# Pairing edge blocks on VectorE in a sparse graph-attention kernel

## The chip, the cores and the metric

The kernel runs on one core of a Trainium2 chip. A core has five engines that run their own queues in order: TensorE (PE in the profile, with its weight loads as PEld), VectorE (DVE), ScalarE (ACT), GpSimd (POOL) and SyncE (SP, which here only issues DMAs). The metric is the device time of one execution in microseconds, as the median over several runs; lower is better.

## The reference, cut to what matters

One layer of graph attention over 16 batches of 1024 nodes with 512 features and 8 heads of 64, followed by the residual and a layer norm. `adj` is the same for all batches, holds zeros and ones, and is sparse: few keys for most queries, many for some.

```python
q = (x @ Wq + bq).reshape(b, n, H, HD)
k = (x @ Wk + bk).reshape(b, n, H, HD)
v = (x @ Wv + bv).reshape(b, n, H, HD)
scores = jnp.einsum('bqhd,bkhd->bhqk', q, k) / jnp.sqrt(jnp.float32(HD))
scores = scores + (1.0 - adj)[None, None, :, :] * -1000000000.0
attn = jax.nn.softmax(scores, axis=-1)
out = jnp.einsum('bhqk,bkhd->bqhd', attn, v).reshape(b, n, d)
...
x = _layernorm(x + out @ Wo + bo)
```

All is float32.

## The kernel before, in words

**The sparse attention.** Instead of scores for all 1024 x 1024 pairs the kernel works on the edges alone. Queries are ranked by their number of keys and laid in 8 tiles of 128. A *block* is 128 edges: on each of the 128 partitions one query and one of its keys. `OWN = (2, 1, 2, 3, 4, 5, 5, 7)` gives the own blocks of each tile, where block i holds the i-th key of the tile's own 128 queries; `BLOCKS` adds one further block for tile 6 and five for tile 7, whose edges belong to arbitrary queries of the tile and are summed back by a matmul with a 0/1 matrix (`sums`). Some tiles with few keys are merged over two batches. In all there are 530 blocks, in the order of the list `blocks`; the blocks of neighbouring places mostly belong to one tile, with the further blocks spread in between.

**A block's life**, each step a function:
- `gather(n)` issues an indirect DMA on POOL that brings the 128 rows `kvg` (512 key and 512 value features, 4 KB a partition) from a table in DRAM; queries come as `qt`, once a tile through SP, or as `qg` for a further block, once a block through POOL.
- `products(n)` (L1313) multiplies queries and keys on VectorE into a tile `qk`.
- `scores(n)` (L1317) sums the product over each head's 64 features on VectorE, 8 values a partition.
- `exponentials(n)` (L1328) takes their exponential on ACT, into the last 8 columns of `pv`.
- `weigh(n)` multiplies the values by it: on ACT in eight pieces (L1341) or on VectorE at once (L1345). `by_act` chooses; 450 blocks go to ACT, 80 to VectorE.
- `add_own(n)` (L1357, VectorE) adds an own block to its tile's sum, or `add_up(n)` (L1366, L1367, PE) does it for a further block.
- `normalise` (L1387, VectorE) divides after a tile's last block, and the result goes through transposes (L1401) to the product with Wo (`po`, L799).

**The dense part.** For the batches to come, PE transposes x (`pxT`, L757) and makes q (`pq`, L799) and, for two tiles of x at a time, k and v by a Strassen-like scheme (L956) with banks `x`, `z` and `pp`; VectorE evacuates and combines (L783 to L786, L972, L975, L979, L984, L988), and ACT evacuates others (L761, L835, L969). The banks `x` and `z` have one buffer each, so the second use of `z` follows the evacuation at L984.

**The order** is written out by hand in one loop over steps n (L1538 to L1623), one block a step, with every engine's instructions issued in this order. In step n stand, one after the other: the exponential of block n + 3, the product of n + 4, the gathers up to n + 8 (11 near the end), VectorE's weighing of n + 1, the addition of n, the sum by heads of n + 4, the normalising of a tile that closed, what was put off to this step (`plan`: evacuations and parts of the layer norm), ACT's weighing of n + 2, more put-off work (`rest`), and then as many units of dense PE work as a running credit allows. Buffers are handed out in rotation by tag: tag "kvg" has 8 buffers of 4 KB a partition, which first hold the 8 tiles of `adj` while the edges are found; tag "kv" has 5, which serve the dense part, and edge blocks too near the end; "qk" has 2 of 2 KB.

A gather into a buffer waits for the weighing that read it last. POOL works in order, so what stands behind a waiting gather waits too.

Of the kernel before, what the change touches and what calls it, by code (L numbers as in the profile page):

```python
# [10 lines left out]
F32 = mybir.dt.float32  # L11
# [3 lines left out]
OP = mybir.AluOpType  # L15
AX = mybir.AxisListType

HEADS = 8
# [8 lines left out]
OWN = (2, 1, 2, 3, 4, 5, 5, 7)  # L27
# [11 lines left out]
PAIRED_FROM, SPARED = 2, 56  # L39
# [35 lines left out]
P = 128  # L75
# [103 lines left out]
def kernel(  # L179
# [36 lines left out]
    nc = tc.nc  # L216
    B, N, D = x.shape
    HD = D // HEADS
    NPAIR = D // P
# [35 lines left out]
    with ExitStack() as main:  # L255
# [380 lines left out]

        def edges(t):
            nb, J, K = BLOCKS[t], DEGREE[t], OWN[t]
            tag, bufs = ("kvg", KG_BUFS) if J > 16 else ("kv", 5)
            v = work.tile([P, N], F32, tag=tag, name=f"codes_{t}", bufs=bufs)  # L640
# [60 lines left out]
            for i0 in range(0, nb, step):  # L701
                n = min(step, nb - i0)
                g0 = first[t] + i0
                pg = fill_psum(f"pe_{t}_{i0}")
                g = pg[:, 0:n * (J + 3)].rearrange("p (n j) -> p n j", n=n)
                for i in range(n):
                    nc.tensor.matmul(g[:, i, :], of[:, ts(i0 + i, P)], kl, start=True, stop=True)
                yield
                e = small.tile([P, 2, n], F32, tag=f"ee{n}", name=f"ee_{t}_{i0}", bufs=1)
                m = work.tile([P, D], F32, tag="qk", name=f"em_{t}_{i0}", bufs=2)[:, 0:n * J].rearrange("p (n j) -> p n j", n=n)  # L710
                nc.vector.tensor_tensor(e[:, 0, :], placed[:, i0:i0 + n], g[:, :, J], op=OP.subtract)
                nc.vector.tensor_tensor(
                    m, place[:, None, 0:J].to_broadcast([P, n, J]), e[:, 0, :, None].to_broadcast([P, n, J]),
                    op=OP.is_equal,
                )
# [485 lines left out]

        KG, QG, PV, PSUM, QT, RDEN, V1 = {}, {}, {}, {}, {}, {}, {}

        def blocks_of(b, t):

# [42 lines left out]
        def gather(n):  # L1250
# [33 lines left out]
            else:  # L1284
# [7 lines left out]
            nc.gpsimd.indirect_dma_start(  # L1292
                out=KG[n], out_offset=None, in_=rows,
# [3 lines left out]

        S = {}

        QK = {}  # L1300

        def products(n):
            b, t, i = blocks[n]
            if t == 0 and i == 0 and b < PAIRED_FROM:
                norms = small.tile([P, NPAIR], F32, tag="lone", name=f"lone_{b}", bufs=1)
                later_last(0, lambda q=QT[b, t]: squares(f"q_{b}", q, norms, lone))
                later(2, lambda: nc.vector.tensor_reduce(lone_norm[:, b:b + 1], norms, axis=AX.X, op=OP.max))
            if i < OWN[t]:
                q = QT[b, t] if i < OWN[t] - 1 else QT.pop((b, t))
            else:  # L1310
                q = QG.pop(n)
            QK[n] = work.tile([P, D], F32, tag="qk", name=f"qk_{n}", bufs=2)
            nc.vector.tensor_tensor(QK[n], q, KG[n][:, 0:D], op=OP.mult)  # L1313

        def scores(n):
            S[n] = small.tile([P, HEADS], F32, tag="s", name=f"s_{n}", bufs=4)
            nc.vector.tensor_reduce(S[n], QK.pop(n).rearrange("p (h d) -> p h d", d=HD), axis=AX.X, op=OP.add)  # L1317

        def exponentials(n):

            b, t, i = blocks[n]
            if i == 0:
                PV[n] = work.tile([P, D + HEADS], F32, tag="pv0", name=f"pv_{n}", bufs=3)
            else:
                PV[n] = work.tile([P, D + HEADS], F32, tag="pv", name=f"pv_{n}", bufs=PV_BUFS)
            at = NK + i if t == 0 and merged(b) else own[t] + i
            bias = absent[:, at:at + 1] if i < OWN[t] else 0.0
            nc.scalar.activation(PV[n][:, D:], S.pop(n), AF.Exp, bias=bias)  # L1328
# [187 lines left out]
        with tc.manual_schedule():  # L1516
# [21 lines left out]
            while n < total or plan or rest or urgent or done or finishing or spilled or lone_tiles or not guarded:  # L1538
# [6 lines left out]
                elif n in start:  # L1545
# [112 lines left out]
```

## Time and profile before

| | us |
|---|---|
| median of 3 runs | 1860.07 |
| lowest and highest run | 1853.99, 1872.71 |
| span of the profiled execution, first to last instruction | 1840.4 |
| the profiled execution's own time | not shown; the runs lie 13.6 to 32.3 above the span |
| VectorE: products, L1313, both forms (x530) | 363.0 |
| VectorE: sums by heads, L1317 (x530) | 360.7 |
| VectorE: additions, L1357 (x329) | 228.3 |
| ACT: weighing, L1341 (x3600) | 907.5 |

The profile's line of a group reads: line, engine, operation, output and inputs by the program's tile names, shapes as partitions x elements, count, then busy time in all, mean of one in ns, and the engine's idle time just before such instructions with what ended it. Busy time of a group is what it adds to the time in which the engine has an instruction running, so where one instruction starts before the last has ended, count times mean is more than busy. The granted clock is the share of full clock that TensorE was given; its mean is 0.996.

### The profile page before, as it was taken

How to read it: one execution, taken by the hardware profiler on the slowest of the kernel's cores; microseconds unless marked ns; L12 is line 12 of the kernel's file. 1: busy time of each engine (PE TensorE's matmuls, PEld its weight loads, DVE VectorE, ACT ScalarE, POOL GpSimd, SP SyncE). 2: the span in 40 equal slices, each digit the busy share in tenths (PEclk: the TensorE clock that was granted, in tenths of full speed). 3: DMA queues.
4: the chain of work that ended last, by engine and by line, in shares of the span. 5: the costliest groups of instructions: out<-in, count | busy, mean ns of one | idle time of the engine just before them, and what ended most of it. 6: DMA issues, size and time to landing. Idle time of an engine off the chain costs nothing.

```text
span 1840.4 us, 25352 instructions
## 1 busy us (share of the span) xinstructions
PE 1798.2 (98%) x5140; PEld 876.2 (48%) x5140; DVE 1693.7 (92%) x3473; ACT 1563.2 (85%) x6183; POOL 1215.3 (66%) x1142
## 2 busy tenths in 40 slices
PE   7999999999999999999999999999999999999997
PEld 3444454554444454444444445444544444444443
DVE  6889889999989999999999999999999999997986
ACT  3637869989889898999889988989799999987886
POOL 1367766766565776767757666677666767665786
PEclk9999999999999999999999999999999999999998
DMA  7358787989889899999988998999989999889995
GB/s 287 106 190 253 256 325 237 346 301 327 308 280 314 295 336 319 344 316 308 347 316 310 346 335 276 343 321 322 339 315 325 314 355 326 306 324 325 338 319 191
DMA packets 198791, 558.54 MB, mean 303 GB/s; under 512 B 33450, under 2 KB 33470, under 8 KB 198626
## 3 DMA queue, kind: packets, MB, share of 16 engines
q0 software_dynamic: 112640, 370.50, 59.3%
q1 hardware_dynamic: 82910, 180.52, 26.2%
q10 hardware_dynamic: 3076, 5.82, 0.9%
q14 instruction: 122, 1.00, 0.2%
q8 instruction: 43, 0.70, 0.2%
HBM read 420.30 MB, written 157.45 MB: 314 GB/s over the span
## 4 chain that ended last, share of the span: by engine, by line
PE 69%; DVE 10%; ACT 9%; DMA 4%; issue 3%; POOL 1%; SPq 0%; POOLq 0%; DVEq 0%; ACTq 0%
PE po L799 17%; PE pq L799 15%; PE pp L956 12%; PE z L956 9%; PE x L956 9%; ACT pv L1341 5%; DVE qk L1313 2%; PE poT L1401 2%; PE pxT L757 2%; PE sum L1367 2%; DVE s L1317 2%; PE sum L1366 2%; DVE pv L1357 1%; ACT sq_k L809 1%; DMA kvg<-kv_pair,place_row 1%
## 5 line engine op out<-in xcount | busy, mean ns | idle before, releaser
L1341 ACT ACTIVATE pv<-kvg,pv 128x64 f32<-128x64 f32 x3600 | 907.5, 341 | 0.0
L1292 POOL DMA_INDIRECT kvg<-kv_pair,place_row x462 | 526.7, 1140 | 307.4 <-ACT pv L1341 99.6
L799 PE MATMUL pq<-wq,xT 128*128 128x512 f32 x792 | 367.8, 596 | 0.0
L1317 DVE TENSOR_REDUCE s<-qk 128x8 f32<-128x512 f32 x530 | 360.7, 681 | 6.8
L799 PE MATMUL po<-wo,oT 128*128 128x512 f32 x792 | 359.3, 594 | 0.7 <-ACT oT L1405 0.7
L1313 DVE TENSOR_TENSOR qk<-qt,kvg 128x512 f32<-128x512 f32 x434 | 297.2, 685 | 1.1 <-DMA kvg<-kv_rows,key_row 0.6
L956 PE MATMUL x<-b,xT 128*128 128x512 f32 x504 | 237.3, 593 | 0.5 <-ACT e L969 0.4
L956 PE MATMUL pp<-t,s 128*128 128x512 f32 x504 | 237.0, 593 | 0.0
L1357 DVE TENSOR_TENSOR pv<-pv,pv 128x520 f32<-128x520 f32 x329 | 228.3, 694 | 4.3 <-ACT pv L1341 4.2
L799 PEld LDWEIGHTS po<-wo,oT 128*128 128x128 f32 x792 | 149.1, 191 | 170.0 <-issue 160.2
L799 PEld LDWEIGHTS pq<-wq,xT 128*128 128x128 f32 x792 | 148.4, 192 | 161.9 <-issue 149.9
L1010 POOL DMA_INDIRECT x<-in_x_dram,asked_row x120 | 133.0, 1108 | 77.8 <-issue 21.3
L1148 POOL DMA_INDIRECT out_dram<-y,asked_row x129 | 146.9, 1139 | 39.1 <-issue 21.2
L1328 ACT ACTIVATE pv<-s,absent 128x8 f32<-128x8 f32 x434 | 127.0, 294 | 44.0 <-DVE s L1317 40.8
L809 ACT ACTIVATE sq_k<-kv 128x128 bf16<-128x128 f32 x512 | 150.8, 301 | 6.4 <-DVE kv L979 3.4
L956 PEld LDWEIGHTS pp<-t,s 128*128 128x128 f32 x504 | 94.7, 191 | 108.1 <-issue 99.4
L956 PEld LDWEIGHTS x<-b,xT 128*128 128x128 f32 x504 | 94.2, 191 | 107.4 <-issue 99.0
L956 PE MATMUL z<-b,s 128*128 128x512 f32 x252 | 119.2, 596 | 7.0 <-DVE kv L984 7.0
L1246 POOL DMA_INDIRECT qg<-q_rows,query_row x96 | 104.4, 1088 | 28.4 <-issue 26.9
L956 PE MATMUL z<-t,s 128*128 128x512 f32 x252 | 118.6, 593 | 0.0
L956 PE MATMUL pp<-t,xT 128*128 128x512 f32 x252 | 118.5, 593 | 0.0
L1134 ACT ACTIVATE y<-y,stats 128x512 f32<-128x512 f32 (+1 forms) x128 | 102.7, 806 | 17.0 <-DVE stats L1129 17.0
(279 smaller groups left out, 2713.0 us busy)
## 6 DMA issues: line engine op xcount, KB each, us to landing
kv_pair<-kv SPq DMA_DIRECT2D x98, 512.0 KB
q_rows<-q SPq DMA_DIRECT2D x106, 256.0 KB
qt<-q_rows SPq DMA_DIRECT2D x98, 256.0 KB
residual<-x SPq DMA_DIRECT2D x83, 256.0 KB
y<-residual SPq DMA_DIRECT2D x83, 256.0 KB
kv_rows<-kv SPq DMA_DIRECT2D x15, 512.0 KB
kvg<-kv_pair,place_row POOLq DMA_INDIRECT x462, 6.9
kv_pair<-kv SPq DMA_DIRECT2D x28, 256.0 KB
```

The costliest lines, as they stand in the source:

```text
L799: nc.tensor.matmul(p, lhs(c), w[:, c, :], start=(c == 0), stop=(c == NPAIR - 1))
L809: nc.scalar.activation(sq, s[:, ts(h, P)], AF.Square, scale=scale, accum_out=sums[:, h:h + 1])
L956: nc.tensor.matmul(R[bank], l[:, ts(c, P)], right[:, c, :], start=(first and c == 0), stop=(c == 1), skip_group_check=True,)
L1010: nc.gpsimd.indirect_dma_start(out=y, out_offset=None, in_=x_rows, in_offset=bass.IndirectOffsetOnAxis(ap=asked_row[:, t:t + 1], axis=0), ...
L1148: nc.gpsimd.indirect_dma_start(out=out_rows[b, t], out_offset=bass.IndirectOffsetOnAxis(ap=rows, axis=0), in_=y, in_offset=None, element_o ...
L1246: nc.gpsimd.indirect_dma_start(out=q, out_offset=None, in_=q_rows[b % ROWS], in_offset=bass.IndirectOffsetOnAxis(ap=rows, axis=0))
L1292: nc.gpsimd.indirect_dma_start(out=KG[n], out_offset=None, in_=rows, in_offset=bass.IndirectOffsetOnAxis(ap=(place_row if b else key_row)[ ...
L1313: nc.vector.tensor_tensor(QK[n], q, KG[n][:, 0:D], op=OP.mult)
L1317: nc.vector.tensor_reduce(S[n], QK.pop(n).rearrange("p (h d) -> p h d", d=HD), axis=AX.X, op=OP.add)
L1328: nc.scalar.activation(PV[n][:, D:], S.pop(n), AF.Exp, bias=bias)
L1341: nc.scalar.activation(pv[:, ts(h, HD)], v[:, ds(D + h * HD, HD)], AF.Copy, scale=pv[:, D + h:D + h + 1])
L1357: nc.vector.tensor_tensor(PV[b, t], PV[b, t], pv, op=OP.add)
```

## The change: blocks two at a time

Blocks 2m and 2m + 1 become a pair.

- Tag "kvg" now has 4 buffers for two blocks each (`PAIR`) in place of 8 single ones: the same memory. While dense work is left every pair lies in one such buffer; near the end two of three pairs do, and the others use two single "kv" buffers.
- `products` handles a pair: one multiplication of 128x1024 where both blocks use the same queries (broadcast over the two), else two of 128x512. The product is written over the keys in the gathered tile; the tiles `qk` are gone.
- `scores` handles a pair: one sum by heads over 128x1024 where the pair lies in one buffer.
- In the loop products and sums come in odd steps only, for blocks n + 3 and n + 4. So an even block's product comes one step later than before and an odd block's in the same step as before. Exponentials come one step later (n + 2), and VectorE's weighing stands before the gathers.
- The `adj` tiles, and the edge codes of the tile with most keys, use the paired buffers; a scratch tile of `edges` moves from tag "qk" to tag "ysq".

```diff
-KG_BUFS, Q_BUFS, QT_BUFS, PV_BUFS, Y_BUFS = 8, 5, 3, 5, 6
+KG_PAIRS, Q_BUFS, QT_BUFS, PV_BUFS, Y_BUFS = 4, 5, 3, 5, 6
...
-                ADJ.append(work.tile([P, N], F32, tag="kvg", name=f"adj_{t}", bufs=KG_BUFS))
+                if t % 2 == 0:
+                    two = work.tile([P, 2, N], F32, tag="kvg", name=f"adj_{t}", bufs=KG_PAIRS)
+                ADJ.append(two[:, t % 2, :])
...
-                m = work.tile([P, D], F32, tag="qk", name=f"em_{t}_{i0}", bufs=2)[:, 0:n * J].rearrange("p (n j) -> p n j", n=n)
+                m = work.tile([P, D], F32, tag="ysq", name=f"em_{t}_{i0}", bufs=1)[:, 0:n * J].rearrange("p (n j) -> p n j", n=n)
...
-            tag, bufs = ("kvg", KG_BUFS) if fronts or n % 5 % 2 == 0 else ("kv", 5)
-            KG[n] = work.tile([P, 2 * D], F32, tag=tag, name=f"kvg_{n}", bufs=bufs)
+            if n % 2 == 0 and (fronts or n // 2 % 3 < 2):
+                PAIR[n] = work.tile([P, 2, 2 * D], F32, tag="kvg", name=f"kvg_{n}", bufs=KG_PAIRS)
+            if n // 2 * 2 in PAIR:
+                KG[n] = PAIR[n // 2 * 2][:, n % 2, :]
+            else:
+                KG[n] = work.tile([P, 2 * D], F32, tag="kv", name=f"kvg_{n}", bufs=5)
...
         def products(n):
...
+            pair = [m for m in (n, n + 1) if m < total]
...
+            if len(pair) == 2 and n in PAIR and q[n] is q[n + 1]:
+                k = PAIR[n][:, :, 0:D]
+                nc.vector.tensor_tensor(k, q[n][:, None, :].to_broadcast([P, 2, D]), k, op=OP.mult)
             else:
...
-            QK[n] = work.tile([P, D], F32, tag="qk", name=f"qk_{n}", bufs=2)
-            nc.vector.tensor_tensor(QK[n], q, KG[n][:, 0:D], op=OP.mult)
+                for m in pair:
+                    nc.vector.tensor_tensor(KG[m][:, 0:D], q[m], KG[m][:, 0:D], op=OP.mult)
...
         def scores(n):
-            S[n] = small.tile([P, HEADS], F32, tag="s", name=f"s_{n}", bufs=4)
-            nc.vector.tensor_reduce(S[n], QK.pop(n).rearrange("p (h d) -> p h d", d=HD), axis=AX.X, op=OP.add)
+            s = small.tile([P, 2, HEADS], F32, tag="s", name=f"s_{n}", bufs=3)
+            pair = [m for m in (n, n + 1) if m < total]
+            if n in PAIR and len(pair) == 2:
+                k = PAIR[n][:, :, 0:D]
+                nc.vector.tensor_reduce(s, k.rearrange("p w (h d) -> p w h d", d=HD), axis=AX.X, op=OP.add)
...
-                if 0 <= n + 3 < total:
-                    exponentials(n + 3)
-                if 0 <= n + 4 < total:
-                    products(n + 4)
+                if 0 <= n + 2 < total:
+                    exponentials(n + 2)
+                if 0 <= n + 3 < total and n % 2:
+                    products(n + 3)
+                if 0 <= n + 1 < total and not by_act(n + 1):
+                    weigh(n + 1)
                 while gathered[0] < min(n + (AHEAD if fronts else AHEAD_LAST) + 1, total) and blocks[gathered[0]][0] in set_up:
                     gather(gathered[0])
                     gathered[0] += 1
-                if 0 <= n + 1 < total and not by_act(n + 1):
-                    weigh(n + 1)
                 if 0 <= n < total and blocks[n][2] < OWN[blocks[n][1]]:
                     add_own(n)
-                if 0 <= n + 4 < total:
-                    scores(n + 4)
+                if 0 <= n + 3 < total and n % 2:
+                    scores(n + 3)
```

More of the change, by code (lines that the diff above doesn't have):

```diff
@@ L638, in edges @@
             nb, J, K = BLOCKS[t], DEGREE[t], OWN[t]
-            tag, bufs = ("kvg", KG_BUFS) if J > 16 else ("kv", 5)
-            v = work.tile([P, N], F32, tag=tag, name=f"codes_{t}", bufs=bufs)
+            if J > 16:
+                v = work.tile([P, 2, N], F32, tag="kvg", name=f"codes_{t}", bufs=KG_PAIRS)[:, 0, :]
+            else:
+                v = work.tile([P, N], F32, tag="kv", name=f"codes_{t}", bufs=5)
             nc.gpsimd.indirect_dma_start(
@@ L1199, in complete @@
                 later(6, alone)
-        KG, QG, PV, PSUM, QT, RDEN, V1 = {}, {}, {}, {}, {}, {}, {}
+        KG, PAIR, QG, PV, PSUM, QT, RDEN, V1 = {}, {}, {}, {}, {}, {}, {}, {}
         def blocks_of(b, t):
@@ L1288, in gather @@
                 gather_q(QG[n], b, (query_row if b else query_row0)[:, g:g + 1])
-            tag, bufs = ("kvg", KG_BUFS) if fronts or n % 5 % 2 == 0 else ("kv", 5)
-            KG[n] = work.tile([P, 2 * D], F32, tag=tag, name=f"kvg_{n}", bufs=bufs)
+            if n % 2 == 0 and (fronts or n // 2 % 3 < 2):
+                PAIR[n] = work.tile([P, 2, 2 * D], F32, tag="kvg", name=f"kvg_{n}", bufs=KG_PAIRS)
+            if n // 2 * 2 in PAIR:
+                KG[n] = PAIR[n // 2 * 2][:, n % 2, :]
+            else:
+                KG[n] = work.tile([P, 2 * D], F32, tag="kv", name=f"kvg_{n}", bufs=5)
             rows, base = (pair_rows[b // 2 % 2], 0) if t == 0 and merged(b) else kv_of(b)
@@ L1298 @@
         S = {}
-        QK = {}
         def products(n):
[L1303 to L1309, printed above, removed]
-            else:
-                q = QG.pop(n)
-            QK[n] = work.tile([P, D], F32, tag="qk", name=f"qk_{n}", bufs=2)
-            nc.vector.tensor_tensor(QK[n], q, KG[n][:, 0:D], op=OP.mult)
+            pair = [m for m in (n, n + 1) if m < total]
@@ new lines, in products @@
+            q = {}
+            for m in pair:
+                b, t, i = blocks[m]
+                if t == 0 and i == 0 and b < PAIRED_FROM:
+                    norms = small.tile([P, NPAIR], F32, tag="lone", name=f"lone_{b}", bufs=1)
+                    later_last(0, lambda q=QT[b, t], norms=norms: squares(f"q_{b}", q, norms, lone))
+                    later(2, lambda b=b, norms=norms: nc.vector.tensor_reduce(lone_norm[:, b:b + 1], norms, axis=AX.X, op=OP.max))
+                if i < OWN[t]:
+                    q[m] = QT[b, t] if i < OWN[t] - 1 else QT.pop((b, t))
+                else:
+                    q[m] = QG.pop(m)
@@ L1315, in scores @@
+            if len(pair) == 2 and n in PAIR and q[n] is q[n + 1]:
+                k = PAIR[n][:, :, 0:D]
+                nc.vector.tensor_tensor(k, q[n][:, None, :].to_broadcast([P, 2, D]), k, op=OP.mult)
+            else:
+                for m in pair:
+                    nc.vector.tensor_tensor(KG[m][:, 0:D], q[m], KG[m][:, 0:D], op=OP.mult)
         def scores(n):
-            S[n] = small.tile([P, HEADS], F32, tag="s", name=f"s_{n}", bufs=4)
-            nc.vector.tensor_reduce(S[n], QK.pop(n).rearrange("p (h d) -> p h d", d=HD), axis=AX.X, op=OP.add)
+            s = small.tile([P, 2, HEADS], F32, tag="s", name=f"s_{n}", bufs=3)
@@ new lines, in scores @@
+            pair = [m for m in (n, n + 1) if m < total]
+            if n in PAIR and len(pair) == 2:
+                k = PAIR[n][:, :, 0:D]
+                nc.vector.tensor_reduce(s, k.rearrange("p w (h d) -> p w h d", d=HD), axis=AX.X, op=OP.add)
+            for m in pair:
+                S[m] = s[:, m - n, :]
+                if n not in PAIR or len(pair) == 1:
+                    nc.vector.tensor_reduce(
+                        S[m], KG[m][:, 0:D].rearrange("p (h d) -> p h d", d=HD), axis=AX.X, op=OP.add
+                    )
@@ L1319, in exponentials @@
+            PAIR.pop(n, None)
         def exponentials(n):
```

## The prediction

> **What bounds the kernel now.** I read the busy shares and the chain first, then PE by stretches of the span, then what PE waited for. The first row gives each engine's busy time, its share of the span and its instructions; the second the engines' shares of the chain that ended last.
>
> ```profile
> PE 1798.2 (98%) x5140; PEld 876.2 (48%) x5140; DVE 1693.7 (92%) x3473; ACT 1563.2 (85%) x6183; POOL 1215.3 (66%) x1142
> PE 69%; DVE 10%; ACT 9%; DMA 4%; issue 3%; POOL 1%; SPq 0%; POOLq 0%; DVEq 0%; ACTq 0%
> ```
>
> Three engines are nearly full, so the share alone settles nothing. By stretches (start and end in us, length, busy time of PE, PEld, DVE, ACT and POOL with counts, granted clock, DMA share, GB/s):
>
> ```profile
> 0.00:100.00 100.00, 89.30 (x238) 42.23 (x239) 74.18 (x165) 48.71 (x120) 28.79 (x48) 0.98 0.53 189
> 100.00:1700.00 1600.00, 1583.24 (x4561) 774.65 (x4560) 1507.68 (x2993) 1405.86 (x5727) 1082.14 (x997) 1.00 0.89 312
> 1700.00:1800.00 100.00, 98.95 (x277) 47.27 (x276) 87.44 (x237) 83.09 (x267) 81.34 (x75) 1.00 0.94 333
> 1800.00:1840.40 40.40, 26.66 (x67) 12.01 (x65) 24.39 (x80) 25.54 (x69) 23.05 (x25) 0.86 0.45 160
> ```
>
> From 100 to 1700 us PE is idle for 1600 - 1583.2 = 16.8 us, DVE for 92.3, ACT for 194. PE's other idle time is 10.7 us at the start, 1.1 from 1700 to 1800 and 13.7 at the end, 42.3 in all. A busy PE could still be a slowed one, so I look at its rate in the chain (start, length, what):
>
> ```profile
> 819.59 3.43 PE pq L799 x8
> ...
> 919.15 3.44 PE pq L799 x8
> ```
>
> A hundred microseconds apart eight matmul records take 3.43 and 3.44 us, 0.43 each, at a granted clock of 1.00. That is PE at its pace, not PE waiting inside a matmul. So TensorE bounds the kernel, and another engine matters where it makes PE wait. Those waits (us in total, times, longest; in the first row the 7.0 us stand behind the bar):
>
> ```profile
> L956 PE MATMUL z<-b,s 128*128 128x512 f32 x252 | 119.2, 596 | 7.0 <-DVE kv L984 7.0
> ...
> PE z L956 <- DVE kv L984: 7.0, 5, 3.0
> PE pm L867 <- DVE vsum L863: 3.1, 3, 1.9
> PE poT L1401 <- DVE stats L1123: 3.1, 1, 3.1
> PE poT L1401 <- DVE o L1387: 2.6, 1, 2.6
> ```
>
> VectorE's waits come to 7.0 + 3.1 + 3.1 + 2.6 = 15.8 us in 10 stalls, 1.6 us each. That sum, not the 1693.7 us of busy VectorE, is what relief of VectorE can reach.
>
> **The change part by part.** *The merged instructions.* The lines that change, with count, busy us, mean ns:
>
> ```profile
> L1317 DVE TENSOR_REDUCE s<-qk 128x8 f32<-128x512 f32 x530 | 360.7, 681 | 6.8
> L1313 DVE TENSOR_TENSOR qk<-qt,kvg 128x512 f32<-128x512 f32 x434 | 297.2, 685 | 1.1 <-DMA kvg<-kv_rows,key_row 0.6 <-DMA kvg<-kv_pair,place_row 0.4
> ...
> L1345 DVE TENSOR_TENSOR pv<-kvg,pv 128x512 f32<-128x512 f32 x80 | 54.9, 686 | 0.0
> ```
>
> 530 blocks make 265 pairs. Walking the block order, 257 pairs lie in one tile (8 of the last ones don't), so 257 sums merge. A multiplication merges only where both blocks use the same queries, that is two own blocks of one tile: 149 pairs. Together 406 instructions go. What one is worth is read from starts on VectorE's timeline:
>
> ```profile
> 1060.05 0.68 DVE L1317 TENSOR_REDUCE s<-qk 128x8 f32<-128x512 f32 x1
> 1060.64 0.15 DVE L1129 SCALAR_TENSOR_TENSOR stats<-stats 112x1 f32<-112x1 f32 x1
> ...
> 1060.77 0.68 DVE L1313 TENSOR_TENSOR qk<-qt,kvg 128x512 f32<-128x512 f32 x1
> 1061.37 0.69 DVE L1345 TENSOR_TENSOR pv<-kvg,pv 128x512 f32<-128x512 f32 x1
> ...
> 1066.34 0.68 DVE L1313 TENSOR_TENSOR qk<-qt,kvg 128x512 f32<-128x512 f32 x1
> 1067.06 0.69 DVE L1317 TENSOR_REDUCE s<-qk 128x8 f32<-128x512 f32 x1
> ...
> 25.04 1.23 DVE L458 MAX8 asked<-keys 128x8 f32<-128x1024 f32 x1
> 26.18 0.41 DVE L783 TENSOR_TENSOR s<-xT 128x256 f32<-128x256 f32 x1
> ...
> 36.38 1.23 DVE L384 TENSOR_TENSOR t<-b,t 128x1024 f32<-128x1024 f32 x1
> 37.52 1.22 DVE L457 TENSOR_TENSOR keys<-adj,place 128x1024 f32<-128x1024 f32 x1
> ```
>
> A 512-wide instruction lasts 0.68 but the next starts 0.59 to 0.60 after it, as long as it doesn't need its result; a sum right behind its own product starts 0.72 after. 1024 wide the step is 1.14, for the two-input operation and for the reducing MAX8, which I take for the wide sum. So one merger saves 2 x 0.60 - 1.14 = 0.06 us: 406 x 0.06 = 24 us. By durations it would be 2 x 0.68 - 1.23 = 0.13, or 53 us; if two rows of 512 inside one instruction cost as two, nothing. I take 24 because starts are what the queue feels; the ends 0 and 53 stay. Second, a sum that stands directly behind its product (neither a weighing nor an addition between) pays 0.72 - 0.60 = 0.12: by the block order 179 times now, 79 after, 12 us. VectorE is relieved of 24 + 12 = 36 us.
>
> [...]
>
> *Later exponentials.* Each now comes one step later on ACT, about where the next block's stands today, while the 80 weighings on VectorE keep their step (an odd block's comes about 0.60 earlier in it, since no product precedes). One such block:
>
> ```profile
> 1028.28 0.29 ACT L1328 ACTIVATE pv<-s,absent 128x8 f32<-128x8 f32 x1
> ...
> 1031.56 0.20 ACT L1328 ACTIVATE pv<-s 128x8 f32<-128x8 f32 x1
> ...
> 1031.84 0.68 DVE L1345 TENSOR_TENSOR pv<-kvg,pv 128x512 f32<-128x512 f32 x1
> ```
>
> Its exponential ended 3.3 us before the weighing; in the next one's place it ends at 1031.56 + 0.29 = 1031.85, the weighing could start at 1031.24, so VectorE waits 0.6, and behind it the addition, the sums and the evacuations. Shifting all 80 in this way, 10 come late, 7 us together; the ends are 0 and 80 x 0.6 = 48. Net relief: 36 - 7 = 29 us, 0.055 per step of 1840.4/530 = 3.5 us. The weighings on ACT already follow the exponential in ACT's own order and don't move.
>
> *The lump.* In an odd step the wide product and sum put everything behind them (normalising, PE's evacuations) 2 x 0.54 = 1.08 us later; in an even step about 1.2 earlier. The tightest consumer is the single z bank:
>
> ```profile
> 1060.99 1.88 PE L956 MATMUL pp<-t,xT 128*128 128x512 f32 x4
> 1065.88 1.98 PE L956 MATMUL z<-b,s 128*128 128x512 f32 x4 [3.01 <-DVE kv L984]
> ...
> 1063.61 0.43 DVE L783 TENSOR_TENSOR s<-xT 128x256 f32<-128x256 f32 x1 [0.35 <-ACT xT L761]
> ...
> 1065.14 0.68 DVE L984 TENSOR_TENSOR kv<-z,g 128x512 f32<-128x512 f32 x1
> ```
>
> This stall is a backlog: four subtractions stood ahead of the evacuation that PE needed. There are 252/4 = 63 such places, 5 stall today, about half fall in odd steps. A backlog that grew over some 20 steps is 20 x 0.055 = 1.1 us shorter, two thirds of a mean stall; where the lump strikes it takes 1.08 back. I take a third of the 15.8 us as gained: 5.3. Ends: all of it (15.8), and 31 odd places each 1.08 late, a loss of 33.
>
> *The gathers.* A pair's buffer comes free when both blocks are weighed, so the even gather, and what follows it on POOL's queue (stores, loads of x, the power of the variance), waits for one more weighing; the odd one then waits for nothing. POOL's waits, the landing times of the gathers (least, median, most), and one even gather with the weighing it would now wait for and its product:
>
> ```profile
> POOL kvg L1292 <- ACT pv L1341: 110.4, 85, 6.2
> ...
> DMA to landing us min/median/max: 3.8/6.8/10.8
> ...
> DVE qk L1313 <- DMA kvg<-kv_pair,place_row: 1.3, 2, 0.8
> ...
> 991.18 1.38 POOL L1292 DMA_INDIRECT kvg<-kv_pair,place_row  x1 [0.30 <-ACT pv L1341]
> ...
> 990.05 2.06 ACT L1341 ACTIVATE pv<-kvg,pv 128x64 f32<-128x64 f32 x8
> ...
> 1000.98 0.68 DVE L1313 TENSOR_TENSOR qk<-qt,kvg 128x512 f32<-128x512 f32 x1
> ```
>
> The gather would go at 992.1 instead of 991.2; at the slowest landing it is there at 1002.9, and its product, one step later than now, is due at about 1004.5. Zero, hidden by the step that the product moves; without that cover it costs 2. SP's loads of queries wait for the last product of an older tile, one step later for even blocks, hidden by the same eight blocks of lead. The adjacency tiles in pairs, the scratch under "ysq" and the fewer score tiles touch a few instructions near the start: zero. The product over the keys waits for nobody, since the keys are read by the product alone.
>
> *Sum.* The profiled execution's span of 1840.4 - 5.3 = 1835.1. Its own time isn't shown; the runs (1853.99 to 1872.71) lie 13.6 to 32.3 above the span, the median 1860.07 lies 19.7 above. With 19.7 around it: 1854.8, so 1855, 0.3% less.
>
> **The rivals.** *VectorE sets the pace.* Its 92% speak for it, and the ten stalls. Then the whole 36 us reach the end: 1824. Against it: PE would have to shed 36 of its 42.3 idle us, of which 24.4 lie at start and end. [...]
>
> *The lump starves the z bank (slower).* Where three quarters of the 31 odd places lose 1.08 us, 23 x 1.08 = 25: 1885. It decides from 18.6/1.08 = 17 places on. For it: PE waits on L984 already. Against: only 5 of 63 do, so most places have room, and even steps gain.
>
> *The wide instruction costs as two.* Then VectorE gains nothing but the 12 us behind products, eaten by the 7: 1860.
>
> **How the numbers follow.** About 1%, 18.6 us, is what a measurement of this kernel can tell from no change; the three runs alone spread 18.7. My forecast 0.67, with its own range 1843 (all 15.8 gained, rounded) to 1868 (a quarter of the loss end); the third rival 0.10; VectorE as bound, or stalls and end shortened together, 0.10; the lump 0.13. Faster by over 1%: 0.10. Within: 0.67 + 0.10 = 0.77. Slower: 0.13. The range reaches halfway to the outer cases, 1838 to 1880, and leaves out about 0.2.
>
> **What would show it.** Right: VectorE's busy time down by 25 to 60 us, wide products and sums of 1.2 us with the next start after 1.14, PE's busy time unchanged within a few us, its waits on L984 and L863 shorter. Wrong: wide sums near 1.36 us; waits of L1345 on exponentials above 15 us; products waiting for gathers; PE's idle time between 100 and 1700 us above 30, above all before z. A time under 1841 would show that PE was not the bound that I read.

## The result, and the profile after

The changed kernel takes 1881.26 us (median of four runs, 1877.38 to 1882.32); the kernel before, run beside it, takes 1859.19 us (four runs, 1853.99 to 1872.71). The ratio is 1.0112, with a 95% interval of 1.0068 to 1.0155: some 1.1% slower, where 0.3% faster was forecast, and just outside the range of 1838 to 1880.

The first two parts of the changed kernel's page answer to the rows shown first in the prediction (busy time, share and instructions of each engine; the engines' shares of the chain that ended last):

```profile
PE 1813.6 (96%) x5140; PEld 877.3 (47%) x5140; DVE 1664.2 (89%) x3064; ACT 1584.9 (84%) x6183; POOL 1238.6 (66%) x1142
...
PE 55%; ACT 16%; DVE 11%; DMA 6%; issue 6%; POOL 3%; another core or an unknown queue 1%; SPq 0%; POOLq 0%; DVEq 0%; ACTq 0%
```

VectorE lost 3473 - 3064 = 409 instructions and 1693.7 - 1664.2 = 29.5 us of busy time. That part of the change does what it says. And yet PE, with the same 5140 records, is busy for 15.4 us longer and fills a smaller part of the chain. The same stretches as before (the last one is longer, since the span is):

```profile
0.00:100.00 100.00, 89.55 (x239) 42.25 (x240) 75.10 (x167) 48.72 (x120) 29.05 (x49) 0.98 0.52 189
100.00:1700.00 1600.00, 1562.63 (x4466) 760.12 (x4465) 1448.15 (x2546) 1398.90 (x5625) 1082.28 (x975) 0.99 0.88 305
1700.00:1800.00 100.00, 95.37 (x260) 44.76 (x259) 83.14 (x191) 73.59 (x248) 71.07 (x66) 0.98 0.92 330
1800.00:1880.50 80.50, 66.08 (x178) 30.17 (x176) 57.84 (x164) 63.64 (x191) 56.18 (x53) 0.95 0.66 231
```

From 100 to 1700 us PE is now idle for 1600 - 1562.6 = 37.4 us (16.8 before), above the 30 that the prediction named as a sign of its being wrong; the granted clock is 0.99 there and not 1.00. What waits (us, times, longest), of PE, VectorE and POOL:

```profile
PE pm L871 <- DVE vsum L867: 6.9, 5, 2.4
...
PE z L960 <- DVE kv L988: 6.3, 5, 3.1
...
POOL kvg L1300 <- ACT pv L1352: 101.9, 51, 8.5
POOL kvg L1300 <- ACT pv L1365: 89.0, 43, 5.5
POOL kvg L1300 <- DVE pv L1369: 41.4, 16, 7.5
...
DVE kvg L1327 <- DMA kvg<-kv_pair,place_row: 14.6, 14, 2.5
```

Products wait for gathers, which they hardly did before (1.3 + 0.6 us), and POOL waits longer for single weighings (7.5 us at most where it was 3.7). PE waits for the z bank no longer than before (6.3 us where it was 7.0), but longer for `vsum`, the sum for the mean (6.9 where it was 3.1). This trace holds about a third fewer semaphore records than the second trace of the same kernel, which follows. The view puts a wait whose record is missing down to "issue", so the sums by cause are lower bounds here.

**Two traces that can be compared.** The trace of before doesn't belong to any of the runs shown, and most likely came from another chip: a run's time is its span and some 1.7 us (1882.24 and 1880.5 in the changed kernel's profiled run), so the span of 1840.4 belongs to a run of about 1842, below every run shown. Chips differ: in the five groups of runs that follow, the kernel before took 1846.58, 1847.75, 1875.04, 1874.47 and 1846.07 us. So both kernels were profiled again, each on one of the quicker chips; spans are 1845.9 and 1867.0. The kernel before, then the changed kernel, first part of the page:

```profile
PE 1799.3 (97%) x5140; PEld 874.4 (47%) x5140; DVE 1693.5 (92%) x3473; ACT 1563.8 (85%) x6183; POOL 1224.1 (66%) x1142
```

```profile
PE 1809.7 (97%) x5140; PEld 877.4 (47%) x5140; DVE 1664.1 (89%) x3064; ACT 1584.8 (85%) x6183; POOL 1237.2 (66%) x1142
```

The 21.1 us between the spans are 10.7 of idle PE (46.6 to 57.3) and 10.4 of busy PE, in which the same matmuls took longer. Of PE's idle time, what ends with VectorE grew from 19.9 us in 14 stalls to 32.7 in 26 (all such rows of the view of waits together), so by more than the whole 10.7. The readings below are made on these two.

### The profile page after: what moved, and what is told of

It is laid out like the page before. It is cut to its first block, busy times and chain, and to the rows that moved or that the text cites. A ratio compares the mean times of both kernels' runs of the same rounds, so it can differ in the third digit from the quotient of the medians.

```text
span 1880.5 us, 24802 instructions
## 1 busy us (share of the span) xinstructions
PE 1813.6 (96%) x5140; PEld 877.3 (47%) x5140; DVE 1664.2 (89%) x3064; ACT 1584.9 (84%) x6183; POOL 1238.6 (66%) x1142
## 4 chain that ended last, share of the span: by engine, by line
PE 55%; ACT 16%; DVE 11%; DMA 6%; issue 6%; POOL 3%; another core or an unknown queue 1%; SPq 0%; POOLq 0%; DVEq 0%; ACTq 0%
PE po L803 13%; PE pq L803 12%; ACT pv L1365 10%; PE pp L960 10%; PE x L960 7%; PE z L960 6%; DMA kvg<-kv_pair,place_row 3%; DVE s L1334 2%; PE poT L1425 2%; ACT sq_k L813 1%; PE pxT L761 1%; PE sum L1391 1%; PE sum L1390 1%; DVE kvg L1327 1%; DVE pv L1381 1%
## 5 line engine op out<-in xcount | busy, mean ns | idle before, releaser
L1300 POOL DMA_INDIRECT kvg<-kv_pair,place_row x462 | 541.5, 1172 | 354.4 <-issue 99.0
L1334 DVE TENSOR_REDUCE s<-kvg 128x16 f32<-128x1024 f32 x259 | 314.1, 1213 | 2.6
L1324 DVE TENSOR_TENSOR kvg<-qt,kvg 128x1024 f32<-128x1024 f32 x150 | 182.7, 1218 | 7.6 <-issue 4.7
L1138 ACT ACTIVATE y<-y,stats 128x512 f32<-128x512 f32 (+1 forms) x128 | 102.3, 803 | 16.6 <-DVE stats L1133 15.5
```

The lines of the kernel that those rows point to most:

```text
L1300: nc.gpsimd.indirect_dma_start(out=KG[n], out_offset=None, in_=rows, in_offset=bass.IndirectOffsetOnAxis(ap=(place_row if b else key_row)[ ...
L1324: nc.vector.tensor_tensor(k, q[n][:, None, :].to_broadcast([P, 2, D]), k, op=OP.mult)
L1334: nc.vector.tensor_reduce(s, k.rearrange("p w (h d) -> p w h d", d=HD), axis=AX.X, op=OP.add)
```

## The experiments

All ratios are to the kernel before on the same chip, with 95% intervals. As a measure of what can be told apart, the kernel before as a run of its own:

> The kernel before as a run of its own: its ratio to itself shows what the measurement tells apart (1.000 within 0.25%), and its trace shows what this chip does to it. Theory: the stalls of PE between 100 and 200 us and the stretches at half clock belong to a chip on which the kernel before takes some 1875 us, and are there without the change as well; on a chip where it takes some 1847 us the trace is as the first one, with 5 us lost in that stretch. Rival: they come with the change alone.

It came out at 1.0003 (0.9992 to 1.0014). The stalls that the expectation names are these: from 100 to 200 us PE is busy for 89.1 us in the first trace of the changed kernel (at a mean granted clock of 0.93), and for 83.5 to 91.0 (0.90 to 0.95) in four kernels on one of the two slower chips (where the kernel before takes 1874 us). The kernel before ran on one of the quicker chips here, and its trace is much as the first one: from 100 to 1700 us PE is busy for 1580.9 us, and for 1583.2 there (96.5 of it from 100 to 200 us). On quicker chips that stretch has 95.2 us of busy PE in the changed kernel too, and 96.0 to 96.1 in two of the kernels that follow. So whether the early stalls belong to the slower chips alone was not settled.

**Four kernels that take the change apart** (on a chip where the kernel before takes 1846.58 us). First, the changed kernel with every wide instruction as two:

```diff
-                nc.vector.tensor_tensor(k, q[n][:, None, :].to_broadcast([P, 2, D]), k, op=OP.mult)
+                for w in range(2):
+                    nc.vector.tensor_tensor(k[:, w, :], q[n], k[:, w, :], op=OP.mult)
```

(and the sum by heads likewise).

> The changed kernel with every wide multiplication and wide sum issued as two of 512: same buffers, same order, only the merging undone. If the buffers in pairs cause the loss (A) or the new order does (B), the time stays at about 1.011 of before or rises by what the 24 to 36 us more of VectorE work cost, 1.010 to 1.02. If the wide instructions themselves cause it (C: they hold VectorE's queue for 1.2 us at a time), it falls back to 1.00.

Measured: 1.0099 (1.0082 to 1.0116), so the wide instructions are not what costs (C falls). VectorE is busy for 1681.3 us, 17.2 more than merged. Second, the kernel before with its gather buffers in pairs, and VectorE's weighing ahead of the gathers as the change has it, but nothing merged or moved otherwise:

```diff
-            KG[n] = work.tile([P, 2 * D], F32, tag=tag, name=f"kvg_{n}", bufs=bufs)
+            if n % 2 == 0 and (fronts or n // 2 % 3 < 2):
+                PAIR[n] = work.tile([P, 2, 2 * D], F32, tag="kvg", name=f"kvg_{n}", bufs=KG_PAIRS)
+            if n // 2 * 2 in PAIR:
+                KG[n] = PAIR[n // 2 * 2][:, n % 2, :]
```

> The kernel before with the gathers' buffers in pairs, and VectorE's weighing ahead of the gathers, nothing else. A (an even gather waits for two weighings, POOL stands still, gathers come late, products wait for them): 1.010 to 1.015. Without the product's extra step for even blocks the hold should hurt even more than in the changed kernel. B or C: 1.00.

Measured: 1.0084 (1.0060 to 1.0107), a little under what A gave. VectorE's largest wait on this path:

```profile
DVE qk L1321 <- DMA kvg<-kv_pair,place_row: 20.8, 19, 3.3
```

Third, the new order with single buffers and nothing merged:

```diff
-                if 0 <= n + 3 < total:
-                    exponentials(n + 3)
-                if 0 <= n + 4 < total:
-                    products(n + 4)
+                if 0 <= n + 2 < total:
+                    exponentials(n + 2)
+                for m in (n + 3, n + 4):
+                    if 0 <= m < total and n % 2:
+                        products(m)
```

(and the sums likewise).

> The kernel before with the new order alone: two products and two sums in each odd step for blocks n + 3 and n + 4, exponentials a step later, single buffers, nothing merged. A: 1.00, or a little below since gathers get a step more. B (the lump in odd steps, and later exponentials, make VectorE late for PE): 1.010 to 1.015, with more waits of PE on VectorE.

Measured: 1.0069 (1.0051 to 1.0087), between what A and B gave. Products hardly wait for gathers; weighings and additions wait for ACT:

```profile
DVE pv L1357 <- ACT pv L1341: 8.0, 12, 2.1
DVE pv L1345 <- ACT pv L1328: 7.1, 9, 1.9
```

Fourth, of that order the exponentials alone (`exponentials(n + 2)` for `exponentials(n + 3)`, one line):

> The kernel before with the exponentials one step later and nothing else. Splits B: if the exponentials carry it, 1.01; if the lump does, or A holds, 1.00 within 0.004.

Measured: 1.0040 (1.0024 to 1.0055), at the edge of the one answer and far from the other:

```profile
DVE pv L1345 <- ACT pv L1328: 5.7, 5, 2.5
DVE pv L1357 <- ACT pv L1341: 4.8, 8, 2.1
```

So no part that was tried gains, and three cost: buffers in pairs 0.84%, the new order 0.69%, in it the exponentials 0.40%. The two large ones would add up to 1.5%; together they cost 0.99%. So the parts hide one another. The 0.84% is that of the buffers together with VectorE's weighing ahead of the gathers; the two were not separated.

**Taking parts away again** (on a chip where the kernel before takes 1847.75 us). The changed kernel again, and the same with both exponentials of a pair in the even step, so that the odd block's is as early as before:

```diff
-                if 0 <= n + 2 < total:
-                    exponentials(n + 2)
+                for m in (n + 2, n + 3):
+                    if 0 <= m < total and n % 2 == 0:
+                        exponentials(m)
```

> The changed kernel once more, beside the variants of it below, so that they have a common measure. Theory: the merging itself is worth about nothing, and the loss is the sum of the buffers in pairs and of the new order; then this kernel stands where its split form stood, 1.009 to 1.012 of the kernel before. Rival: the merged instructions themselves cost (or gain), and this kernel stands over 0.4% away from 1.010. [...]

> The changed kernel with both exponentials of a pair in the even step: the odd block's is as early as in the kernel before, the even block's as in the changed kernel. Theory: the later exponential cost 0.40% when put into the kernel before alone; half of the blocks get their slack back, so that VectorE's waits of a weighing on an exponential fall from 4.4 us to under 2 and the ratio falls by 0.1 to 0.4%, to 1.007 to 1.010. Rival: two exponentials in a row hold ScalarE's other work up, and the ratio stays at 1.011 or more.

Measured: 1.0110 (1.0083 to 1.0137) and 1.0105 (1.0086 to 1.0124). Merged the ratio is 1.0110 and split it was 1.0099; the intervals overlap, so the 17.2 us that merging takes off VectorE brought nothing that can be measured. While gathers are late, earlier exponentials bring nothing that can be measured either, although the weighings' waits for exponentials fell from 5.6 to 2.2 us; 1.0105 lies between what the theory and the rival gave.

The other half was to give each gather buffer back by itself, with the merging kept: `kvg` as one tile of eight slots, and the gathers ahead of VectorE's weighing again. In its first form the codes of a whole adjacency tile lost their slot too soon, and the kernel's guard sent the work to its general path (17088 us, and 17077 with the exponentials moved as well): of the change these two tell nothing. In the second form the codes have a tile of their own (on a chip where the kernel before takes 1875.04 us); near the end a few of the 530 blocks read the rows of other blocks, so that results are wrong while the instructions stay the same:

```diff
-                PAIR[n] = work.tile([P, 2, 2 * D], F32, tag="kvg", name=f"kvg_{n}", bufs=KG_PAIRS)
+                PAIR[n] = next_pair()
...
+        ring = work.tile([P, 2 * KG_PAIRS, 2 * D], F32, name="kvg", bufs=1)
```

> The changed kernel, merging and order kept, with the gather buffers as eight slots of one tile (each half given back by its own weighing; the adjacency codes of one tile of rows in a tile of their own). Theory: the odd gather stands no longer behind a held even one; VectorE's waits on gathers fall from 17 us to under 6, and the ratio to the kernel before falls from 1.011 to 1.003 to 1.007. Rival: the loss lies in the merging or in the later exponentials; the waits on gathers may fall, but the ratio stays at 1.009 to 1.012.

> The slots of one tile, and both exponentials of a pair in the even step (the odd block's as early as in the kernel before). Theory: 0.1 to 0.3% under the kernel with the slots alone, 1.000 to 1.005 of the kernel before. Rival (the exponentials cost only where a single weighing follows at once, as the pair form alone without the slots, 1.0105 against 1.011, suggests): the same as the slots alone within 0.1%.

> The slots of one tile, with the merged products and sums one step earlier, in even steps for the blocks four and five ahead, and every exponential in the step that it had in the kernel before: no exponential is late, but an odd block's gather has three steps and not four to land (9.3 us by 3.1 us a step, where landings took 6.8 us in the middle and 10.8 at the longest). Theory (merging neutral, loss from exponentials and gathers): the waits on exponentials vanish, those on gathers grow to 10 to 30 us; 0.998 to 1.006. Rival (the lump of a merged product and sum holds up what PE waits for on VectorE): 1.006 or more with PE's waits on VectorE above 20 us.

> The kernel before with its single buffers and unmerged instructions, two products and two sums in odd steps and none in even ones, both exponentials in the even step behind them: an odd block's exponential as early as before, an even block's one step later. Theory: it lies between the kernel before and the new order with every exponential late (1.0069), at 1.002 to 1.005, as half of the exponentials have their slack back. Rival (the lump itself is what the order costs): 1.006 to 1.008.

Measured: 1.0088 (1.0067 to 1.0110) with the slots, 1.0047 (1.0024 to 1.0070) with the exponentials moved too, 1.0136 (1.0105 to 1.0168) with products one step earlier, where gathers are late again (35.6 us, above what the theory gave, and PE's waits for VectorE are above 20 as the rival has it), and 1.0044 (1.0021 to 1.0067) for the unmerged order with the exponentials moved. The first is above what the theory gave. The second and the last have the same order, one merged and one not, on one chip, and can't be told apart; their intervals leave room for a difference of some 0.3%.

Since the changed kernel had not run beside these, the slots were made again, on a chip where the kernel before takes 1874.47 us; a slot is now taken only when its reader has been issued, so every block reads its own rows, and the last of the four has nine slots:

```diff
+        def free(n):
+            return not ringed(n) or HOLDS.get(next_slot()) not in KG
...
-                PAIR[n] = work.tile([P, 2, 2 * D], F32, tag="kvg", name=f"kvg_{n}", bufs=KG_PAIRS)
...
+                KG[n] = ring[:, at, :]
+                if n % 2 and at == SLOT[n - 1] + 1:
+                    PAIR[n - 1] = ring[:, at - 1:at + 1, :]
```

> The changed kernel once more, as the measure for the three beside it on the same chip: 1.009 to 1.013 of the kernel before, as on two other chips.

> The changed kernel with the gather buffers as eight slots of one tile, each given back by its own weighing (no gather is issued into a slot that the program still reads). Theory (buffers in pairs and later steps each take slack away, and what is late counts once, by whichever is later): the gathers' waits vanish but the exponentials are still late, so only part comes back, 1.006 to 1.010, at least 0.1% under the changed kernel beside it. Rival (the buffers cost nothing while the steps are late): the same as the changed kernel within 0.1%.

> The slots, with both exponentials of a pair in the even step. Theory: 1.002 to 1.006, clearly under the slots alone, although the same shift of the exponentials with buffers in pairs gave only 0.05%. Rival (exponentials cost nothing): the slots' own ratio.

> Nine slots and gathers nine blocks ahead, merged products and sums in even steps for the blocks four and five ahead, exponentials where the kernel before has them: gathers have four steps and more, as before, exponentials are not late, and only the merging and the lump of a wide product and a wide sum in every second step are left of the change (and an unmerged pair where slots wrap, one in nine). Theory (what is late is all that costs): VectorE's waits on gathers under 5 us, none on exponentials, and 0.997 to 1.002. Rival (the lump holds up what PE waits for on VectorE): 1.004 or more, with PE's waits on VectorE above those of the kernel before (17 us).

Measured: the changed kernel 1.0065 (1.0039 to 1.0092), below what was expected; with slots 1.0066 (1.0044 to 1.0089), where the rival was right and not the theory; with slots and the moved exponentials 1.0016 (0.9993 to 1.0039); with nine slots 1.0049 (1.0028 to 1.0069). The traces of this chip, and those of the other slower one, lack a third of the semaphore records like the first trace of the changed kernel. What needs no such record is VectorE's idle time right before products, weighings and additions, whatever ended it: 37.0 us in the changed kernel, 19.6 with slots, 11.3 with the moved exponentials too and 11.5 with nine slots (8.5 in the kernel before on a quicker chip). With the slots alone VectorE's waits on gathers are gone (1.8 us in all), but those on ACT are not, and the time stays:

```profile
DVE pv L1396 <- ACT pv L1380: 8.3, 12, 2.1
DVE pv L1384 <- ACT pv L1367: 4.9, 3, 2.0
...
DVE kvg L1342 <- DMA kvg<-kv_pair,place_row: 1.1, 1, 1.1
DVE kvg L1339 <- DMA kvg<-kv_rows,key_row: 0.7, 1, 0.7
```

With the exponentials moved as well both are small, and the kernel can't be told from the one before:

```profile
DVE pv L1396 <- ACT pv L1380: 5.3, 8, 1.8
...
DVE pv L1384 <- ACT pv L1367: 2.2, 2, 1.5
DVE kvg L1339 <- DMA kvg<-kv_rows,key_row: 0.9, 1, 0.9
```

So late exponentials alone are enough for the loss on this chip, as late gathers were on another with the exponentials moved (1.0105, above). Without both it is gone in this kernel, but not in every one: the forecast for nine slots (0.997 to 1.002) was missed with hardly anything late, PE still waits 35.4 us for VectorE there, and the rival's 1.004 was right. Its waits are no full answer either, since they are 30.0 us in the kernel at 1.0016. That kernel was not run on a quicker chip, where the changed one loses more (1.0110).

Last, the wide sum was taken out of the odd step, to the head of the even one (on a chip where the kernel before takes 1846.07 us):

```diff
+                if 0 <= n + 2 < total and n % 2 == 0:
+                    scores(n + 2)
                 for m in (n + 2, n + 3):
...
-                if 0 <= n + 3 < total and n % 2:
-                    scores(n + 3)
```

> The slots and the exponentials in even steps, with the lump taken apart: the wide product stays in the odd step, the wide sum goes to the head of the even step that follows, ahead of both exponentials. Theory (with the waits gone, the lump of 2.4 us in one step is what is left, 0.2 to 0.5%): 0.996 to 1.001, the merging's relief of VectorE at last visible or at least nothing lost. Rival (the lump costs nothing, but the exponentials now wait for the sum): 1.002 to 1.006, with weighings on VectorE waiting over 5 us for exponentials.

Measured: 1.0066 (1.0048 to 1.0084). The theory fell; the rival's time (1.002 to 1.006) is just missed, and its sign, weighings waiting for exponentials above 5 us, isn't there either (2.5). PE's waits show what came:

```profile
PE z L960 <- DVE kv L988: 5.3, 2, 3.0
PE poT L1440 <- DVE stats L1127: 4.1, 1, 4.1
PE pb L410 <- DVE q L834: 3.7, 1, 3.7
PE po L803 <- DMA oTs<-spill: 3.0, 1, 3.0
...
PE pm L871 <- DVE vsum L867: 2.4, 2, 1.9
```

The wait for `vsum` is 2.4 us where it was 6.5 (changed kernel, another of the quicker chips); single stalls at other places took its place.

**What roughly lines the runs up** is how long VectorE itself waits on the edges' path. Below, for the runs on the quicker chips, are all its waits for gathers (`kvg`) and for ACT's `pv`, with PE's waits for VectorE, both summed over the rows of the views of waits:

| kernel | VectorE waits, us | PE waits for VectorE, us | ratio |
|---|---|---|---|
| before | 8.3 | 19.9 | 1.0003 |
| exponentials later | 12.8 | 24.1 | 1.0040 |
| slots, wide sum in the even step | 14.3 | 23.0 | 1.0066 |
| new order, unmerged | 18.6 | 28.7 | 1.0069 |
| buffers in pairs | 28.7 | 23.4 | 1.0084 |
| changed, split | 33.9 | 29.5 | 1.0099 |
| changed, exponentials moved | 37.0 | 31.9 | 1.0105 |
| changed | 43.1 | 32.7 | 1.0110 |

The order is no proof: most neighbours' intervals overlap, and a trace shows one execution while the ratio is that of a median. The trace of the buffers in pairs is of the shortest of its four runs (1853.49 us, 1.0037), which is less than its row would have it. On the slower chips, whose sums are lower bounds, the order is rougher, from 1.0016 to 1.0049 at 7 to 12 us of such waits, 1.0047 to 1.0088 at 18 to 30, and 1.0136 at 45. No kernel beat the kernel before.

## Why the prediction was wrong, step by step

**PE as the bound, and what relief of VectorE can reach.** Right: 29.5 us less of busy VectorE brought no time, and the rival in which VectorE sets the pace (1824) is refuted. The 15.8 us were the four largest rows; all of VectorE's rows in that view are 18.1 us in 13 stalls.

**The merged instructions.** Right in kind, the size too large. The prediction had 406 mergers at 0.06 us, 24 us, and 12 more from the order. Measured: 409 mergers (259 wide sums, 150 wide products), 17.2 us by merging (split against merged, 0.042 each) and 12.2 by the order (split against before). VectorE's timeline of the changed kernel (start, length) gives the steps as forecast:

```profile
1559.95 1.23 DVE L1324 TENSOR_TENSOR kvg<-qt,kvg 128x1024 f32<-128x1024 f32 x1
1561.22 1.22 DVE L1334 TENSOR_REDUCE s<-kvg 128x16 f32<-128x1024 f32 x1
1562.36 0.19 DVE L1410 RECIPROCAL rden<-pv 128x8 f32<-128x8 f32 x1
1562.58 0.69 DVE L1411 TENSOR_TENSOR o<-pv,rden 128x512 f32<-128x512 f32 x1
```

The next start is 1.14 us after the wide sum's, and 1.27 after the wide product's, whose result the sum needs. The rival "the wide instruction costs as two" falls.

**The gathers: the first step that failed.** The prediction put them at "Zero, hidden by the step that the product moves", and had the odd one "then waits for nothing". It followed an even block, whose product does move a step. The odd block's product keeps its step, and its gather now stands on POOL's queue behind the even one, which waits for both weighings. Over 440 blocks (numbers 40 to 479, in the first trace of each kernel) an even gather was issued 12.5 us ahead of its product and is so now (12.5); an odd one was 12.4 us ahead and is 10.1, in a twentieth of the cases 7.3 or less, while the 333 landings that the first trace of the kernel before shows take 6.8 us in the mean, over 9.0 in a twentieth and 10.8 at the longest. An odd product can come too late, and it does: VectorE's waits on gathers are 4.1 us in the kernel before and 29.1 in the changed one. The largest row of each:

```profile
DVE qk L1313 <- DMA kvg<-kv_pair,place_row: 3.8, 4, 1.4
```

```profile
DVE kvg L1327 <- DMA kvg<-kv_pair,place_row: 15.6, 14, 2.2
```

The buffers in pairs (with the weighing ahead of the gathers) cost 0.84% without anything else of the change, 15.5 us, where the prediction had "without that cover it costs 2". The slots took the waits away, but not the loss as long as the exponentials were late (1.0065 and 1.0066): this step alone does not make the whole.

**The later exponentials: the second step that failed.** Their size as waits was right (10 late weighings, 7 us in all; measured alone 5 and 5.7 us). What failed is the next line, "Net relief: 36 - 7 = 29 us": busy time saved and waiting time added were set off against each other. Alone the exponentials add 4.5 us of waits on VectorE (8.3 to 12.8 in the table) and cost 0.40%, 7.4 us; 17.2 us saved in 409 pieces brought nothing that can be measured. A likely reason, not shown on its own: a piece of 0.04 us can disappear in VectorE's own idle time, while a wait of 1 or 2 us can stand whole in front of an evacuation.

**The lump.** "I take a third of the 15.8 us as gained: 5.3" had the wrong sign. The rival named the lump, and its time (1885) lies near the result, but its place was wrong: the z bank is not starved (8.4 us in 5 stalls before, 8.4 in 4 now). The lump strikes where VectorE's work has PE waiting one or two instructions on: at the sum for the mean. The same place in the kernel before and in the changed kernel, PE and VectorE on the timeline:

```profile
1365.88 0.69 DVE L1357 TENSOR_TENSOR pv<-pv,pv 128x520 f32<-128x520 f32 x1
1366.49 0.67 DVE L1317 TENSOR_REDUCE s<-qk 128x8 f32<-128x512 f32 x1
1366.81 1.02 PE L799 MATMUL pq<-wq,both 128*128 128x512 f32 x2
1367.09 1.40 DVE L863 TENSOR_TENSOR vsum<-vsum,kv 128x512 f32<-128x512 f32 x2
...
1368.55 1.02 PE L867 MATMUL pm<-vsum,mean 128*1 128x512 f32 x2 [0.71 <-DVE vsum L863]
```

```profile
1376.08 0.68 DVE L1327 TENSOR_TENSOR kvg<-qg,kvg 128x512 f32<-128x512 f32 x1
1376.64 1.02 PE L803 MATMUL pq<-wq,both 128*128 128x512 f32 x2
1376.68 0.69 DVE L1381 TENSOR_TENSOR pv<-pv,pv 128x520 f32<-128x520 f32 x1
1377.29 1.21 DVE L1334 TENSOR_REDUCE s<-kvg 128x16 f32<-128x1024 f32 x1
1378.42 1.41 DVE L867 TENSOR_TENSOR vsum<-vsum,kv 128x512 f32<-128x512 f32 x2
...
1379.88 1.02 PE L871 MATMUL pm<-vsum,mean 128*1 128x512 f32 x2 [2.22 <-DVE vsum L867]
```

Before, an addition and a single sum stand ahead of the sum for the mean; now a second product and the second half of a wide sum do so as well, and PE's stall is 2.22 us and not 0.71. PE's wait for `vsum` is 2.3 to 3.7 us in the four kernels without the lump in odd steps on the quicker chips (before, exponentials alone, pairs alone, wide sum moved) and 5.8 to 8.0 in the four with it, merged or not. So the wait comes with the lump; what it is worth in time isn't shown, since other stalls came when it was taken apart.

**Busy PE.** The sum held it constant. It grew by 10.4 us, half of the loss. Part of it goes with the granted clock: its mean is 0.996 over the 1845.9 us of the kernel before and 0.992 over the 1867.0 of the changed one, so 7.4 and 14.9 us of full clock were not granted. The difference makes an estimate of some 7 of the 10.4 us, good to 2 us, as the means are rounded, and rather too high, as it takes in time in which PE was idle. About 2 of the 7 lie in the first 100 us, at 0.98 where it was 1.00; the first trace of the kernel before has 0.98 there as well. The rest is open. What follows a stall can be slower as well: behind the stall of 2.22 us shown above six matmuls for q took 4.54 us, and behind that of 0.71 us the same six took 2.84.

**The base.** The prediction put 19.7 us around the span; it is 1.7, and the span came from a quicker execution. So the time of 1855 says little by itself; the ratio, 1.011 where 0.997 was forecast, is the error. The prediction also took 1%, 18.6 us, for what a measurement can tell from no change; the intervals above reach 0.1 to 0.4% to either side.

What stays open: the 0.2 to 0.7% of the kernels in which hardly anything on the edges' path is late. They differ from the kernel before in the order of VectorE's work, and PE waits for VectorE in 13 to 21 stalls, at other places in each; no single one was shown to be the cause. That the early stalls of the slower chips are there without the change was not tested on such a chip.

## What to carry to other kernels

Busy time saved on an engine that isn't the bound can be worth nothing, while a wait added on it can come back as time: here 17.2 us saved on VectorE by merging brought nothing that can be measured (1.0110 merged, 1.0099 split), 4.5 us of waits came with 7.4 us of time, and 34.8 with some 20. So the two must not be set off against each other. When two buffers become one, follow the second of them on the queue that fills it, not only the first. Parts of a change that make the same work late hide each other: to find a cause, add each part alone to the kernel before, for taking one away from the changed kernel may show nothing, as the slots and the earlier exponentials did here.

## What the hardware showed

The same four matmuls took longer behind one stall of TensorE than behind another that was no shorter. In the trace of before PE stood still for 3.01 us ahead of a z matmul and the four that followed took 1.98 us (1065.88, quoted in the prediction). The same place in the second profile of the same kernel:

```profile
1069.03 3.60 PE L956 MATMUL z<-b,s 128*128 128x512 f32 x4 [2.95 <-DVE kv L984]
```

The four took 3.60 us, after a stall of 2.95. The four microseconds around them, first trace and second (the granted clock is the third figure from the end of the row):

```profile
1065.00:1069.00 4.00, 3.12 (x8) 1.45 (x9) 3.81 (x7) 1.59 (x5) 3.09 (x4) 1.00 0.93 292
```

```profile
1068.00:1072.00 4.00, 2.97 (x4) 1.32 (x5) 2.86 (x5) 1.80 (x6) 3.09 (x4) 0.66 1.00 288
```

The mean granted clock of the four microseconds is 1.00 in the first trace and 0.66 in the second. What decides whether the granted clock falls behind a stall was not shown.

Of seven runs of the kernel before on one chip the shortest took 1841.41 us at a mean granted clock of 0.998 and the longest 1849.74 at 0.993; 0.005 of some 1845 us makes an estimate of 9.2, and the spread is 8.3. On another chip the two go together less well: 1844.39 us at 0.995 and 1846.79 at 0.998.
